# One layer of a graph network on one core: the filters' transforms cut into eight small products side by side, and the opening planned together with the odd products

## The chip, the cores and the metric

One core of a Trainium2 chip. The metric is device time in microseconds (us) of one execution; the time of a kernel is the median of several runs. The core has five engines with one instruction stream each: TensorE (PE in the profile; its weight loads are PEld), VectorE (DVE), ScalarE (ACT), GpSimd (POOL) and SyncE (SP). Each stream runs in the order in which it was written. Transfers are started by SP, ACT or POOL and run on 16 DMA engines.

## The reference

All data are float32. `x` is (64, 256, 256): 64 graphs of 256 nodes with 256 features. Cut to what matters:

```python
h = maximum(layernorm(x), 0)
# ref(h, adj, weights):
c = relu(bn1(conv1x1(h^T)))                    # 256x256
c = bn2(conv1d(c, conv2_w, padding=8))         # 17 taps, 256x256 channels, along the 256 nodes
x_conv = relu(c + h^T)^T
s = h @ w_se.T + b_se                          # 3 numbers a node
A = exp(-|s_i - s_j|^2) * adj
x_nmp = A @ relu(h @ w_msg.T + b_msg)
g = GRU cell (input [x_conv, x_nmp], state h)  # w_ih (768 x 512), w_hh (768 x 256)
out = x + g
```

## The kernel before

**The work.** Graphs are taken in 32 pairs, four pairs to a block, eight blocks. For a pair the kernel computes hT (the normalized features, channels on partitions), the message product, the affinity matrix, their product, and the gates of the cell. The convolution of 17 taps is done once per block for its eight graphs, in a transformed domain: the 256 nodes are 16 groups of 16, and the transform along a group has 16 complex bins (made by additions on DVE, `Fft.odd` for the upper half of the tree and `Fft.even` for the lower). In each bin the convolution is a 256 x 256 product of channels, done with three real products (kinds 0, 1, 2), 47 products in all (bin 15 has two). Bins 0 to 7 are the odd ones: `begin(0..3)` and `complete(0..3)` do their 24 kinds. Bins 8 to 15 follow in `begin(4..7)` and `complete(4..7)`.

**The filters.** For these products the 17 taps of each of 256 x 256 filters must be transformed into 47 numbers. That is done once, in the opening, on TensorE: `points` holds the transform's constants, `taps` the filters as they lie in memory, and `filters` (before: lines 854 to 864) multiplies them. Seven input channels (KG = 128 // 17) stand together on 119 partitions, and `points` is block-diagonal for them. The 16 bins are done in three passes of 6, 6 and 4 bins, so one step gives 126 or 77 rows of 512 numbers; 19 groups of channels (the last with two) times three passes are 57 steps. Each step is two matmuls (one for each half of the input channels), one ScalarE copy out of PSUM to a ring of eight tiles `fo`, and one transfer to a DRAM tensor `filt`, one for each pass. SP and POOL take turns in starting the transfers. The products read their weights back from `filt`: `load_kinds` starts one transfer of 256 KB for each kind into nine slots `wb`, on SP; each finished product frees a slot and starts the next.

**The opening** before the first product is: load x for pairs 0 to 3 and the taps; `norm`, `transpose_h`, `conv1`, `split` for each of the four pairs, with some filter steps after each; `forward(0)` and `forward(1)`, the additions of the transform for the first and second half of the block, odd then even for each; filter steps; `message(0)`, `embed(0)`, `affinity(0)` among the rest of the filter steps. Two names recur below: `embed` makes zT, the operand with 9 rows in each 32-row quadrant, and `affinity` multiplies zT with itself, a matmul of 9 rows for each of four row groups. At the very start TensorE runs 24 products of zeros (WARM).

**What sets the order.** All these calls are recorded by `Recorder`, line 371, and not issued at once: every engine instruction has line 371 in the profile, so it is found by the tiles it touches. `emit` plans what has been recorded: a list scheduler with a cost for each instruction (in `record`) and due times that come from TensorE's order in the program, and then issues it. What is recorded after an `emit` comes after all of what was before it, on each engine. Before, the first `emit` stands after the last filter step, ahead of the loop over blocks; the second ends the kernel. The tiles of the opening (`stage`: taps, fo, points) are freed after the first `emit`, and the tiles of the loop (`late`: Yv, w_x, xnm, gn, tr, back, hh, halves) take their place.

**In the first block** the loop then does `begin(0)`, `begin(1)`, `complete(0)`, `complete(1)`, `fft.branch_back`, `begin(2)`, ... , `fft.odd_back`, `aggregate(0)`; then loads w_hh and w_ih on POOL and combines them in `weight_sums` (12 additions and changes of sign on DVE). `q_back`, `p_back` and `join` on DVE end the transform. The first product of the gates that needs the convolution is in the trace "acc<-Yv,w_ih".

Of the kernel before, what the change touches and what calls it, by code (L numbers as in the profile page):

```python
# [249 lines left out]
class Recorder:  # L250
# [83 lines left out]
    def record(self, engine, op, args, kw):  # L334
# [3 lines left out]
        n = 1  # L338
# [13 lines left out]
        elif engine == "tensor":  # L352
            cost = n / 597 + 0.006
            if op == "transpose":
                cost = out.shape[-1] / 1170
            elif args[1].shape[0] < 32:
                cost = 0.23
        elif engine == "vector":
            cost = {"bn_stats": 0.33, "bn_aggr": 0.07}.get(op, n / 960 + 0.07)
            if op == "tensor_mul" and n == 256:  # L360
                cost = 0.5
        elif engine == "scalar":
            cost = n / 1400 + (0.2 if op == "activation" else 0.12)
            if out.dtype == U16:
                cost = n / 860
            elif len(out.shape) == 3 and op == "activation" and n == 256:
                cost = 0.49
        else:
            cost = 1.1 if self.planned == 0 else 7.0 if ALU.pow in args else 2.0
# [117 lines left out]
def kernel(  # L487
# [53 lines left out]
    def keep(name, *dims):  # L541
        return const.tile([P, *dims], FP, name=name)
# [24 lines left out]
    st, mv, rstd, shift = (Ring(keep(f"{name}{k}", *dims) for k in range(2)) for name, dims in (  # L567
        ("st", (G * MC, 6)), ("mv", (G * MC, 2)), ("rstd", (G * MC,)), ("shift", (G * MC,))))
    SLOTS = 9
    WARM = 24  # L570
    slots = [keep(f"wb{k}", DC, D) for k in range(SLOTS)]
    aux = Ring(psum.tile([P, W], FP, name=f"aux{k}") for k in range(4))
    acc = Ring(psum.tile([P, 2, W], FP, name=f"acc{k}") for k in range(2))
# [4 lines left out]
    adjh = keep("adjh", 2 * MC * W // 2).bitcast(U16).rearrange("p (k w) -> p k w", w=W)  # L578
    IN = ("h", "xc", "xn")

    U, V = (Slots(t, GB * DC, L // 2, NW) for t in (Ut, Vt))
    PT, Sv, T = (Slots(t, GB * DC, L // 4, NW) for t in (PTt, Svt, Tt))
    Yu = V
# [63 lines left out]

    KG = P // TAPS  # L650
    NG = -(-P // KG)
    FULL = NG - 1
    MAIN = KG * TAPS // 16 * 16
    PARTS = [(0, FULL // 6), (FULL // 6, FULL // 3), (FULL // 3, FULL)]


    PASSES = [range(0, 6), range(6, 12), range(12, 16)]
    taps = stage.tile([KG * TAPS, NG, DC, D], FP, name="taps")
    evicted = Ring(stage.tile([P, W], FP, name=f"fo{k}") for k in range(8))
    bank_points = [filter_points(p, TAPS) for p in PASSES]  # L660
    points = [stage.tile([P, KG * f.shape[1]], FP, name=f"points{n}") for n, f in enumerate(bank_points)]

    def load_taps(dc, a, b, eng):
        v = c2_wT[dc * P + a * KG:dc * P + b * KG].rearrange("(g k) t o -> (k t) g o", k=KG)
        eng.dma_start(out=taps[:MAIN, a:b, dc, :], in_=v[:MAIN])

    def load_last_taps(dc, eng):
        v = c2_wT[dc * P:dc * P + FULL * KG].rearrange("(g k) t o -> (k t) g o", k=KG)
        eng.dma_start(out=taps[MAIN:KG * TAPS, :FULL, dc, :], in_=v[MAIN:])

    def load_last_group(dc, eng):
        last = c2_wT[dc * P + FULL * KG:(dc + 1) * P]
        eng.dma_start(out=taps[:last.shape[0] * TAPS, FULL, dc, :], in_=last.rearrange("k t o -> (k t) o"))

    def load_points(n, eng):
        f = bank_points[n]
        m = np.zeros((P, KG, f.shape[1]), np.float32)
        for k in range(KG):
            m[k * TAPS:(k + 1) * TAPS, k] = f
        eng.dma_start(out=points[n], in_=tc.nc.inline_tensor(m.reshape(P, -1), name=f"points{n}").ap())  # L680


    ROWS = {}
# [13 lines left out]
    nc.scalar.dma_start(out=w_c1, in_=c1_wT.rearrange("(k p) o -> p k o", p=P))  # L697
    for j in range(PB):
        load_x(j)
    load_points(0, nc.scalar)  # L700
    for dc, eng in ((0, nc.sync), (1, nc.scalar)):
        load_taps(dc, *PARTS[0], eng)
        load_last_taps(dc, eng)
    for n in range(1, len(PASSES)):
        load_points(n, nc.scalar)
    for part in PARTS[1:]:
        load_taps(0, *part, nc.sync)
        load_taps(1, *part, nc.scalar)
    load_last_group(0, nc.sync)
    load_last_group(1, nc.scalar)  # L710
    nc.first = None
    nc.gpsimd.memset(Z, 0.0)
    nc.gpsimd.memset(Z[:, 0, :, 2 * SE:KD], 1.0)
# [135 lines left out]

    filt = [dram.tile([P, f.shape[1], DC, D], FP, name=f"filt{n}") for n, f in enumerate(bank_points)]

    def filters(p, m, g, eng):

        kinds = filt[m].shape[1]
        size = min(KG, P - g * KG)
        for dc in range(DC):
            mm(p[:size * kinds, dc * D:(dc + 1) * D], points[m][:size * TAPS, :size * kinds],
               taps[:size * TAPS, g, dc, :], start=dc == 0, stop=True, skip_group_check=True)  # L860
        t = evicted()
        nc.scalar.copy(t[:size * kinds], p[:size * kinds])
        eng.dma_start(
            out=filt[m][g * KG:g * KG + size].rearrange("k t c o -> (k t) (c o)"), in_=t[:size * kinds])


    free = deque(range(SLOTS))
# [8 lines left out]
    def load_kinds(count=SLOTS):  # L876
        for _ in range(count):
            if not (free and pending):
                return
            n, kind = pending.popleft()  # L880
            WB.append((free.popleft(), n, kind))
            m = n // len(PASSES[0])
            nc.sync.dma_start(out=slots[WB[-1][0]], in_=filt[m][:, 3 * (n - PASSES[m][0]) + kind])


    def operands(n):
# [314 lines left out]
            nc.gpsimd.dma_start(out=row_tile(y, g), in_=rows(x, G * i + g), accum_op=ALU.add)  # L1201
            nc.gpsimd.dma_start(out=rows(out, G * i + g), in_=row_tile(y, g))

    FIRST = PARTS[1][1]
    steps = deque((m, g) for g in range(FIRST) for m in range(len(PASSES)))
    steps.extend((m, g) for m in range(len(PASSES)) for g in range(FIRST, NG))
    banks = [0]

    def filter_steps(n):
        for _ in range(n):  # L1210
            banks[0] += 1
            p = acc()[:, 0] if banks[0] % 3 == 0 else aux()
            filters(p, *steps.popleft(), nc.gpsimd if len(steps) % 2 else nc.sync)

    norm(0)
    bn1 = columns("bn1")
# [14 lines left out]
    for t, v in ((b_msg[:, :D], msg_b), (b_msg[:, D:], se_b)):  # L1231
        nc.gpsimd.dma_start(out=t, in_=bass.AP(tensor=v.tensor, offset=v.offset, ap=[[0, P], [1, v.shape[0]]]))
    nc.sync.dma_start(out=w_msg[:, :, :D], in_=msg_wT.rearrange("(k p) o -> p k o", p=P))
    load_adj(0, nc.sync)
    load_x(PB)
    forward(0)
    forward(1)
    filter_steps(len(steps) - (NG - FIRST) - 4)
    pending.extend(TURNS)
    load_kinds()  # L1240
    message(0)
    filter_steps(8)
    embed(0)
    filter_steps(4)
    affinity(0)
    filter_steps(len(steps))
    nc.emit()
    stage_ctx.close()
    late = ctx.enter_context(tc.tile_pool(name="late", bufs=1, reuse_waits="tile"))
    Yvt = late.tile([P, SL], FP, name="Yv")  # L1250
    Yv = Slots(Yvt, GB * DC, L // 2, NW)
    w_x = late.tile([P, 3, len(IN), 3, P], FP, name="w_x")
    xnms = Ring(late.tile([P, DC, W], FP, name=f"xnm{k}") for k in range(2))
    gn_tile, tr_tile = (late.tile([P, DC, W], FP, name=n) for n in ("gn", "tr"))
    back = late.tile([P, DC * W], FP, name="back")
    hh, halves = (late.tile([P, 2 * MC, W], U16, name=n) for n in ("hh", "halves"))
    for b in range(NB):
        i = b * PB
        nxt = i + PB
# [18 lines left out]
            norm(nxt)  # L1278
        fft.branch_back(Yv, T, 2)
        fft.odd_back(Yv, T)  # L1280
        aggregate(i)
        begin(4)
        begin(5)
# [159 lines left out]
```

## Time and profile before

| | us |
|---|---|
| median of 3 runs | 1715.54 |
| lowest and highest of these | 1710.89, 1717.69 |
| profiled execution, its own time | 1717.68 |
| span of its profile (first to last instruction) | 1715.9 |
| PE busy in the span | 1670.4 (97%) |
| DVE busy | 1462.3 (85%) |
| ACT busy | 1040.0 (61%) |
| PE's share of the chain that ended last | 81% |
| DVE's share of it | 11% |
| mean granted TensorE clock | 0.991 |
| first product of the block (acc<-Sv,wb) starts | 97.47 |
| first product of the gates on the convolution (acc<-Yv,w_ih) starts | 166.16 |

A matmul of float32 stands as two records in the trace[...] and a record's end is modelled, so that records overlap. What a matmul takes is read from the distance between starts: two 256-column matmuls, four records, start 0.86 us before the next thing. Times below are us from the span's start.

### The profile page before, as it was taken

Reading aid. Unit: us, or ns where it says so; the run is one execution under the profiler, and the core shown is the slowest. Engines: PE = TensorE matmul, PEld = TensorE weight load, DVE = VectorE, ACT = ScalarE, POOL = GpSimd, SP = SyncE. Lnnn points to the kernel's source line nnn. Section 1 sums busy time; section 2 is a strip of 40 time slices with the busy share of each in tenths; the row PEclk is TensorE's granted clock in tenths of the full one; section 3 lists DMA queues with packets and bytes.
Section 4 is the critical chain, followed back from the end, with each engine's and each line's share of the span. In section 5 each row is a group of like instructions: output and inputs, shape, how many; then the busy total and the mean of one; then the engine's idle time right before and its main releaser. Section 6 shows DMA issues by size and latency. Waiting matters only on the chain.

```text
span 1715.9 us, 26176 instructions
## 1 busy us (share of the span) xinstructions
PE 1670.4 (97%) x8998; PEld 1418.1 (83%) x8998; DVE 1462.3 (85%) x3400; ACT 1040.0 (61%) x1949; POOL 229.8 (13%) x246
## 2 busy tenths in 40 slices
PE   8999999999999999999999999999999999999996
PEld 5788878988789788888888887897888988898885
DVE  7969989798897898898987988978988889879553
ACT  3545665576656756576655766567566665557543
POOL 3210021012110221102110031102211021100000
PEclk9999999999999999999999999999999999999998
DMA  9883665885568465784568645794758846374122
GB/s 217 263 267 121 124 129 117 279 157 127 111 167 254 103 142 99 231 207 97 120 115 271 153 98 119 157 272 99 139 106 218 225 91 135 62 251 113 24 51 50
DMA packets 326457, 260.90 MB, mean 152 GB/s; under 512 B 204808, under 2 KB 252196, under 8 KB 326323
## 3 DMA queue, kind: packets, MB, share of 16 engines
q1 hardware_dynamic: 293818, 213.72, 48.2%
q0 software_dynamic: 29568, 42.84, 13.5%
q10 hardware_dynamic: 2937, 2.66, 0.7%
q8 instruction: 71, 1.16, 0.3%
q14 instruction: 63, 0.52, 0.1%
HBM read 156.03 MB, written 43.78 MB: 116 GB/s over the span
## 4 chain that ended last, share of the span: by engine, by line
PE 81%; DVE 11%; DMA 4%; ACT 3%; issue 1%; POOL 0%; SPq 0%; ACTq 0%; DVEq 0%; POOLq 0%
PE acc L371 56%; PE aux L371 25%; DVE V L371 2%; DVE T L371 2%; DVE tr L371 1%; DVE U L371 1%; DMA wb<-filt 1%; DMA filt<-fo 1%; DMA hh<-halves 1%; ACT gn L371 1%; DVE acc L371 1%; ACT zT L371 1%; DVE e L371 1%; DVE Yv L371 1%; DVE gn L371 1%
## 5 line engine op out<-in xcount | busy, mean ns | idle before, releaser
L371 PE MATMUL acc<-wb,w_ih 128*128 128x256 f32 x768 | 192.4, 379 | 0.0
L371 PEld LDWEIGHTS acc<-wb,w_ih 128*128 128x128 f32 x768 | 145.9, 190 | 19.8
L371 POOL DMA_DIRECT2D back<-in_x_dram x62 | 61.8, 1154 | 717.1 <-ACT back L371 713.8
L371 PE MATMUL acc<-wb,w_x 128*128 128x256 f32 x576 | 137.5, 383 | 11.5 <-DVE acc L371 11.5
L371 PE MATMUL aux<-wb,w_x 128*128 128x256 f32 x576 | 141.9, 384 | 2.3 <-ACT e L371 2.3
L371 DVE SCALAR_TENSOR_TENSOR V<-T,V 128x128 f32<-128x128 f32 (+2 forms) x448 | 140.6, 375 | 0.0
L371 PEld LDWEIGHTS acc<-wb,w_x 128*128 128x128 f32 x576 | 107.3, 190 | 38.1 <-DVE acc L371 19.8
L371 POOL TENSOR_TENSOR rstd<-rstd,neg_half 128x4 f32<-128x4 f32 x32 | 76.9, 2404 | 442.7 <-DVE shift L371 251.3
L371 PEld LDWEIGHTS aux<-wb,w_x 128*128 128x128 f32 x576 | 107.8, 191 | 22.4 <-ACT e L371 4.3
L371 PE MATMUL aux<-w_msg,hT 128*128 128x259 f32 x512 | 121.1, 381 | 2.7 <-ACT fo L371 2.7
L371 PE MATMUL acc<-V,wb 128*128 128x128 f32 x1024 | 117.7, 275 | 0.9 <-DMA wb<-filt 0.9
L371 PEld LDWEIGHTS acc<-U,wb 128*128 128x128 f32 x1024 | 117.1, 192 | 0.9
L371 PE MATMUL acc<-U,wb 128*128 128x128 f32 x1024 | 117.2, 275 | 0.0
L371 PEld LDWEIGHTS acc<-V,wb 128*128 128x128 f32 x1024 | 116.0, 192 | 1.3 <-DMA wb<-filt 1.3
L371 ACT COPY back<-gn 128x1024 uint16<-128x1024 uint16 x62 | 81.0, 1348 | 54.1 <-DMA gn<-back 54.1
L371 PE MATMUL acc<-Yv,w_ih 128*128 128x256 f32 x384 | 110.1, 382 | 0.9 <-ACT Yv L371 0.8
L371 PEld LDWEIGHTS aux<-w_msg,hT 128*128 128x128 f32 x512 | 96.3, 189 | 17.5 <-ACT fo L371 3.1
L371 PE MATMUL acc<-wb,w_hh 128*128 128x256 f32 x384 | 109.9, 381 | 0.0
L371 PE MATMUL aux<-hT,w_c 128*128 128x512 f32 x224 | 105.4, 594 | 2.1 <-DVE msg L371 1.6
L371 PE MATMUL acc<-hT,w_hh 128*128 128x256 f32 x384 | 105.9, 383 | 0.7 <-ACT acc L371 0.7
L371 PE MATMUL aux<-e,msg 128*128 128x256 f32 x448 | 104.4, 379 | 0.0
L371 PE MATMUL acc<-xnm,w_ih 128*128 128x256 f32 x384 | 104.4, 380 | 0.0
(179 smaller groups left out, 3768.0 us busy)
## 6 DMA issues: line engine op xcount, KB each, us to landing
wb<-filt SPq DMA_DIRECT2D x376, 256.0 KB
back<-in_x_dram POOLq DMA_DIRECT2D x62, 256.0 KB, 7.8
out_dram<-back POOLq DMA_DIRECT2D x62, 256.0 KB, 4.8
x<-in_x_dram SPq DMA_DIRECT2D x58, 256.0 KB
halves_d<-halves SPq DMA_DIRECT2D x28, 512.0 KB
adjh<-halves_d SPq DMA_DIRECT2D x112, 128.0 KB
hh<-halves SPq DMA_DIRECT2D x108, 128.0 KB
filt<-fo SPq DMA_DIRECT2D x18, 252.0 KB
```

The source lines that it names most:

```text
L371: self.tasks.append(Task(engine, lambda: method(*args, **kw), cost, size, self.first))
```

## The change

- The filters' transforms. The taps now lie with their 17 taps on partitions, four times (RG = 4) at partitions 0, 32, 64 and 96; quarter r holds 16 input channels (PIECE) of channels 64r to 64r + 63. There are four pieces in a ring of two tiles. A step takes four channels of each quarter: eight matmuls with 17 rows, 64 output rows (47 used and one spare are kept, the rest are zeros) and 512 columns; each has its own quarter of rows and its own half of the output partitions. All 16 bins are done in one step, so 16 steps replace 57. The results go to one `acc` (two banks) and two `aux` banks.
- Ahead of the eight, each step has one full 128 x 128 product of 512 columns of w_c1 with itself. Its result is overwritten. It waits for all that the eight wait for.
- The copies out of PSUM: one of 1024 columns and two of 512 a step, in place of one of 512 for each old step. Four transfers of 192 KB a step, from 48 partitions each, two on SP and two on POOL, in place of one of up to 252 KB. The ring of eight tiles is made of `e_tile`, `adjh`, four quarters of Yv, and two tiles of its own.
- `filt` is one DRAM tensor, so a load of any kind depends on the last step's rows.
- The taps' loads: for each piece four transfers of 16 partitions x 16 KB on SP, and four of one partition x 16 KB on ACT or POOL, in place of transfers of 112 and of 7 partitions. Pieces 2 and 3 are loaded when a tile is free.
- The transforms of the data are recorded odd for both halves, then even for both; all filter steps that are left stand ahead of `message(0)`.
- `load_adj(0)` and `load_x(PB)` are planned after the loads of the first nine kinds. After `affinity(0)` six full products of w_c1 with itself follow.
- The first `emit` is moved into the loop's first pass, after `odd_back`: the odd products are planned with the opening. Yv becomes a tile of its own from the start.
- The plan's cost of a matmul of fewer than 32 rows becomes 0.13 where its output isn't 256 wide. WARM goes from 24 to 35.

```diff
-    KG = P // TAPS
...
+    RG = P // Q
+    HALF = P // 2
+    PIECE = 16
+    KINDS = 3 * BINS
+    taps = Ring(stage.tile([P, PIECE, D], FP, name=f"taps{k}") for k in range(2))
+    lent = [e_tile.rearrange("p g c n -> p (g c n)"), adjh.rearrange("p k w -> p (k w)").bitcast(FP)]
+    lent += [Yvt[:, k * 2 * W:(k + 1) * 2 * W] for k in range(4)]
...
+    def load_taps(eng=nc.gpsimd):
+        t, a = taps(), len(PIECES) * PIECE
+        for r in range(RG):
+            v = c2_wT[r * HALF + a:r * HALF + a + PIECE].rearrange("k t o -> t k o")
+            nc.sync.dma_start(out=t[r * Q:r * Q + L], in_=v[:L])
+            eng.dma_start(out=t[r * Q + L:r * Q + TAPS], in_=v[L:])
+        PIECES.append(t)
...
-    def filters(p, m, g, eng):
-
-        kinds = filt[m].shape[1]
-        size = min(KG, P - g * KG)
-        for dc in range(DC):
-            mm(p[:size * kinds, dc * D:(dc + 1) * D], points[m][:size * TAPS, :size * kinds],
-               taps[:size * TAPS, g, dc, :], start=dc == 0, stop=True, skip_group_check=True)
-        t = evicted()
-        nc.scalar.copy(t[:size * kinds], p[:size * kinds])
-        eng.dma_start(
-            out=filt[m][g * KG:g * KG + size].rearrange("k t c o -> (k t) (c o)"), in_=t[:size * kinds])
+    filt = dram.tile([P, KINDS, DC, D], FP, name="filt")
+
+    def filters(n):
+
+        k, first = n * 4, len(nc.tasks)
+        t, ps, fs = PIECES[k // PIECE], [], []
+        for h in range(2):
+            ps.append([aux(), aux()] if h else acc())
+            fs.append(evicted())
+        mm(ps[0][:, 0], w_c1[:, 0, :P], w_c1.rearrange("p k o -> p (k o)"), start=True, stop=True)
+        for h in range(2):
+            for c in range(DC):
+                rows_r = slice((2 * c + h) * Q, (2 * c + h) * Q + TAPS)
+                for q in range(2):
+                    mm((ps[h][c] if h else ps[h][:, c])[q * HALF:(q + 1) * HALF], points[rows_r],
+                       t[rows_r, k % PIECE + 2 * q:k % PIECE + 2 * q + 2].rearrange("t k o -> t (k o)"),
+                       start=True, stop=True, skip_group_check=True)
...
+        nc.scalar.copy(fs[0].rearrange("p k c o -> p c k o"), ps[0].rearrange("p c (k o) -> p c k o", k=2))
+        for c in range(DC):
+            nc.scalar.copy(fs[1][:, :, c], ps[1][c].rearrange("p (k o) -> p k o", k=2))
+        for h, f in enumerate(fs):
+            for q in range(2):
+                a = h * HALF + k + 2 * q
+                (nc.gpsimd if h else nc.sync).dma_start(
+                    out=filt[a:a + 2].rearrange("k s c o -> s k (c o)"),
+                    in_=f[q * HALF:q * HALF + KINDS].rearrange("p k c o -> p k (c o)"))
...
-    forward(0)
-    forward(1)
-    filter_steps(len(steps) - (NG - FIRST) - 4)
+    for kind in (0, 1):
+        for k in range(2):
+            forward(k, (kind,))
+    filter_steps(len(steps))
     pending.extend(TURNS)
     load_kinds()
+    nc.behind = nc.last["sync"]
+    load_adj(0, nc.sync)
+    load_x(PB)
+    nc.behind = None
     message(0)
-    filter_steps(8)
     embed(0)
-    filter_steps(4)
     affinity(0)
-    filter_steps(len(steps))
-    nc.emit()
...
+    p = aux()
+    for _ in range(6):
+        mm(p, w_c1[:, 0, :P], w_c1.rearrange("p k o -> p (k o)"), start=True, stop=True)
     for b in range(NB):
...
         fft.odd_back(Yv, T)
+        if b == 0:
+            nc.emit()
+            stage_ctx.close()
+            late = ctx.enter_context(tc.tile_pool(name="late", bufs=1, reuse_waits="tile"))
```

## Prediction

> **What bounds the kernel now.** I read the page's first part (PE 97%, DVE 85% of the span), then each engine's busy time by stretches of the opening, TensorE's timeline, the groups of instructions by form, and DVE's waits. Stretches first; columns are length, busy us of PE, PEld, DVE, ACT and POOL with counts, granted TensorE clock, busy share of the DMA engines, GB/s.
>
> ```profile
> 6.00:12.60 6.60, 3.98 (x35) 3.61 (x34) 3.19 (x13) 0.20 (x1) 4.38 (x9) 1.00 1.08 238
> 12.60:19.40 6.80, 6.23 (x13) 3.20 (x13) 5.80 (x27) 0.00 (x0) 3.52 (x6) 0.50 1.12 174
> ...
> 84.40:91.20 6.80, 6.59 (x28) 3.13 (x26) 6.48 (x24) 4.99 (x14) 1.57 (x3) 1.00 0.87 296
> 91.20:98.00 6.80, 6.80 (x21) 4.30 (x21) 4.44 (x17) 2.64 (x7) 1.80 (x3) 0.50 0.61 190
> 98.00:128.00 30.00, 30.00 (x235) 28.61 (x234) 18.34 (x35) 13.35 (x33) 3.11 (x4) 1.00 0.85 283
> 128.00:164.50 36.50, 36.15 (x255) 31.81 (x254) 36.22 (x76) 18.98 (x41) 1.30 (x2) 1.00 0.47 146
> 164.50:246.00 81.50, 80.12 (x363) 65.36 (x361) 78.61 (x185) 54.40 (x102) 13.43 (x12) 1.00 0.61 124
> ```
>
> Three things are to be seen. TensorE is nearly always busy, so work taken from it counts. It ran two stretches of 6.8 us at half clock, each with 3.4 us of work in it less than it could hold; before the second it was busy 6.59 of 6.80 us, but with products of 77 output rows. And from 128 to 246 DVE is as full as TensorE (36.2 of 36.5, 78.6 of 81.5): what TensorE gains in the opening is worth only what DVE can follow. DVE's busy time to 164.5 sums to 135.95 us, so it was idle 28.5 us. Its waits to 166, and TensorE's timeline:
>
> ```profile
> DVE msg L371 <- PE aux L371: 8.4, 3, 7.9
> DVE x L371 <- POOL rstd L371: 5.4, 1, 5.4
> DVE st L371 <- DMA x<-in_x_dram: 4.1, 2, 3.7
> DVE st L371 <- DMA T<-in_x_dram: 3.4, 2, 1.9
> DVE V L371 <- ACT h L371: 2.3, 1, 2.3
> ```
>
> ```profile
> 86.27 0.69 PE L371 MATMUL aux<-zT 9*128 9x256 f32 x2
> 86.89 1.09 PE L371 MATMUL acc<-taps,points 119*77 119x256 f32 x4
> ...
> 90.10 0.70 PE L371 MATMUL aux<-zT 9*128 9x256 f32 x4
> 90.73 0.66 PE L371 MATMUL acc<-taps,points 34*22 34x256 f32 x2
> ...
> 96.62 1.06 PE L371 MATMUL aux<-taps,points 119*77 119x256 f32 x2
> 97.47 2.20 PE L371 MATMUL acc<-Sv,wb 128*128 128x128 f32 x16
> ```
>
> The second list (start, length, records; two records a matmul) says that the first product follows the last filter matmul at once: weights were there, TensorE's own work was not done. It also prices small row groups: one zT matmul takes 0.62 us to the next start, two take 0.63.
>
> [...] at 352.32 us four zT matmuls take 0.65 us[...] One zT matmul alone takes 0.62 us where one of 256 columns in full rows takes 0.43 (0.86 for two). [...] the rate fell to 123 GB/s (8 to 10.4 us), against 282 in the 3 us before. [...]
>
> **The change, part by part.**
>
> *Filters on TensorE.* Removed: 57 steps x 2 matmuls x 0.43 us = 49.0 us. Added: 16 full products x 0.86 (twice 0.43) = 13.8 us, and the small ones. Eight at once would take two halves of 0.43 us (half of a full one's 0.86) and what the zT group pays over a full 256-column matmul, 0.65 - 0.43 = 0.2, or half of that for 64 weight columns in place of 128: 0.96 to 1.07; I take 1.0. If column halves do not overlap it is 2.0, if nothing does 6.9. But the built order shows early groups pulled apart: in nine steps, between conv1 and transposes, small ones stand in pairs or alone, about 19 groups; the last ten steps' worth stand as five pairs, about 10 groups. Each group pays 1.0 whatever it holds: 29 us. Six more full products after the affinity: 5.2 us. Sum 48.0, nearly what was removed. Both half-clock stretches gone would save 6.8 us; the longer warm-up (11 x 0.22 = 2.4 us) lies in the wait for x and closes most of the hole behind the first. A new stretch of small lone products can bring one back. So TensorE's own gain is 49.0 + 6.8 - 48.0 = 7.8 us; bounds: 3.4 us less for every new half-clock stretch.
>
> *When products can start.* conv1(0) ends at 20.7 before; now two small products stand ahead of it that need taps at about 16 us, with a faster clock after: 20.5. From there TensorE has conv1(1..3) 12 x 0.86 = 10.3, transposes 24 x 0.11 = 2.7, full 13.8, groups 29: 76.3. Waits for ScalarE's copies (per step about 0.92 + 2 x 0.49 = 1.9 us, just above TensorE's half of a pair) and for the third and fourth piece of taps: I add 4, so filters end at 80. Then, where messages and affinity formerly lay beside filters, they stand alone: message 3.5, DVE and ScalarE 1.7, z 0.4, zT's copies 2.6 (3.8 from z to zT before, shared with other copies), zT 0.6, six full products 5.2. Products start at 94, 3.5 us earlier. The six hide the write and reload of the last filters; without cover that would be 6.0 (landing of filt) + 3 = 9, to 89 + ScalarE 2 = 91.
>
> *DMA.* [...] By 85 us some 20 MB must have moved, 235 GB/s on average; before, 0 to 97.5 moved 239. So DMA is close to binding[...].
>
> *Odd products planned with the opening.* Before, 24 odd kinds took 97.5 to 128.7, because aggregate, message(1), transposes and zT stood between; now they are alone: 24 x 0.91 = 21.9 us (64 records in 7.3 us before, 8 kinds). Last Yv at 94 + 21.9 + 1.2 = 117. Then DVE: second branch 7.0, odd_back 7.7, and 27 to the scaling of the first xc, relu: 160 against 166.2 for the first gate product on the convolution. DVE alone: it needs 135.95 - 6.2 (nine operations, most of weight_sums, now stand behind that point in its order) = 129.7 of work, plus idle: 11 to the first conv1, 14 waiting for conv1(1..3), which TensorE now reaches some 17 us later because filter groups stand between, 1 for POOL's power: 156. So the products bind by a little, not DVE.
>
> *What is late next.* The 6.2 us of weight sums are then still to do and the gates need them; TensorE covers some with its first gate products (some 12 matmuls before w_x is needed in full); I charge 1 to 6, take 1.5. So 166.2 - 160 - 1.5 = 4.7, say 5 us. After 166 the same work is left and both engines are full, so nothing gives it back.
>
> POOL gets 32 filter writes in place of 28 and 8 taps loads (0.53 us each): hidden, POOL is 13% busy. SP's load_adj(0) and load_x(4) wait behind the loads of weights; the affinity's multiplication then stands ahead of nothing urgent. w_hh and w_ih are loaded some 5 us later on POOL, 15 us ahead of their use.
>
> **Sum.** Profiled execution: 1717.7 - 5 = 1712.7. The median stood 2.1 below it: 1710.5, rounded to 1710.
>
> **Rivals.** (1) *More is gained*: [...] conv1 comes as early as before, so DVE idles only 11 + 3 + 1 and TensorE's products start at 88. For it: TensorE's gain was computed with every lone product paying in full. [...] Gates at 150 to 153, 10 to 16 us earlier: 1702. (2) *DMA becomes the bound, slower*: [...] every product needs the last step's rows. It decides once the last write lands after 99 us (then products start after 101, the first gates after 167); at 109[...], the gates start near 175: 1723. For it: the drop to 123 GB/s. [...] (3) *Column halves do not run side by side*, or clocks halve twice more: 14 or 7 us on TensorE, products at 101 to 108: 1715 to 1724.
>
> **How the numbers follow.** Forecast 0.43 (1706 to 1714), rival 1 0.32, rival 2 0.14, rival 3 0.11. About 0.5% (8.6 us) is what a measurement of this kernel can tell from no change. Faster by more: most of rival 1 and the forecast's edge, 0.38. Slower by more: the far half of rivals 2 and 3, 0.17. Same: 0.45. Range 1697 to 1725: rival 1 to its end, rival 2 to its price, with one in ten left on each side.
>
> **What would show it.** Right: eight small records start within some 0.1 us where they stand together, 1.0 us a group; no half-clock stretch before 98; acc<-Sv,wb near 94, acc<-Yv,w_ih near 160 with DVE full between 85 and 160. Wrong: small groups at 2 us; filt landing after 99; conv1 of the fourth pair before 45 us (rival 1); DVE waiting for Yv by more than 8 us.

## The result, and the profile after

The kernel after takes 1764.6 us (median of 4 runs, 1760.74 to 1766.59) against 1715.1 before: a ratio of 1.0288, 95% interval [1.0261, 1.0316]. It is slower by 49 us, where 1710 had been forecast. Its profiled execution took 1760.74 us, with a span of 1759.0.

| us from the start | before | predicted | after |
|---|---|---|---|
| conv1 of the fourth pair ends | 39.7 | some 57 | 73.6 |
| last filter product starts | 97.0 | ends 80 | 109.2 |
| first product (acc<-Sv,wb) | 97.5 | 94 | 127.2 |
| last odd product ends | 128.2 | 116 | 156.5 |
| first gate product (acc<-Yv,w_ih) | 166.2 | 160 | 203.4 |
| end of the profiled execution | 1717.7 | 1712.7 | 1760.7 |

The loss is made in the opening: 29.8 us by the first product and 37.3 by the first gate product, of 43.1 between the two profiled executions. First the stretches of the kernel after, as in the prediction (length, then busy time of PE, PEld, DVE, ACT and POOL, the granted clock, DMA share, GB/s):

```profile
12.60:19.40 6.80, 4.82 (x20) 2.19 (x19) 6.43 (x26) 0.59 (x1) 3.33 (x7) 1.00 1.17 119
20.00:40.00 20.00, 20.00 (x58) 6.60 (x56) 9.90 (x22) 6.22 (x9) 3.13 (x6) 0.74 0.68 107
40.00:60.00 20.00, 20.00 (x56) 5.45 (x55) 7.74 (x12) 6.71 (x10) 2.83 (x6) 0.66 0.30 80
60.00:80.00 20.00, 20.00 (x93) 7.03 (x86) 12.45 (x37) 7.96 (x13) 4.97 (x9) 0.83 0.88 173
...
98.00:128.00 30.00, 25.87 (x111) 12.53 (x110) 20.48 (x69) 13.13 (x31) 6.61 (x12) 0.80 0.69 206
128.00:164.50 36.50, 31.63 (x254) 29.83 (x253) 20.63 (x45) 10.08 (x18) 3.84 (x5) 1.00 0.94 308
164.50:246.00 81.50, 81.22 (x431) 67.85 (x430) 77.39 (x162) 51.74 (x110) 9.60 (x8) 0.98 0.38 101
```

The early hole is shut: the clock is 1.00 from 12.6 to 19.4, where it was 0.50. But from 20 to 80 us TensorE is busy all the time at a clock of 0.66 to 0.83, and the others are largely idle. From 40 to 60 us it has 56 records, DVE is busy 7.7 of 20 us, and DMA's share is 0.30. Before, the same 20 us were:

```profile
40.00:60.00 20.00, 20.00 (x93) 16.24 (x91) 19.94 (x65) 13.41 (x23) 6.27 (x12) 1.00 0.75 206
```

TensorE is full and does little. What DVE waits for in the kernel after, up to 203 us, says the same (in total, times, longest):

```profile
DVE V L371 <- ACT h L371: 28.7, 3, 12.3
DVE T L371 <- ACT Yv L371: 10.3, 2, 9.3
DVE e L371 <- DMA adj<-in_adj_dram: 6.8, 2, 5.9
```

It waited 28.7 us for conv1 (h), 2.3 before. TensorE's timeline of the kernel after shows why (start, length, records; two records a matmul). The clock stood at half from 24.9 to 35.2 us and from 42.0 to 55.6:

```profile
23.35 1.07 PE L371 MATMUL aux<-taps,points 17*64 17x512 f32 x2
24.35 0.33 PE L371 MATMUL aux<-ident,T 128*128 128x128 f32 x1
...
27.29 1.97 PE L371 MATMUL aux<-taps,points 17*64 17x512 f32 x4
...
43.10 0.47 PE L371 MATMUL aux<-ident,Sv 128*128 128x128 f32 x1
43.50 1.96 PE L371 MATMUL aux<-taps,points 17*64 17x512 f32 x2
45.40 0.47 PE L371 MATMUL aux<-ident,Sv 128*128 128x128 f32 x1
45.80 1.96 PE L371 MATMUL aux<-taps,points 17*64 17x512 f32 x2
...
117.33 2.86 PE L371 MATMUL aux<-zT 9*128 9x256 f32 x8 [0.77 <-ACT zT L371]
120.12 7.28 PE L371 MATMUL aux<-w_c 128*128 128x512 f32 x12
127.23 1.95 PE L371 MATMUL acc<-Sv,wb 128*128 128x128 f32 x16
```

One small product alone between two transposes takes 1.9 us at half clock from its start to the next start; two together (27.29) take the same. At full clock one alone takes 1.0 us (23.35 to 24.35), and a whole group of eight no longer (0.86 us in e10 below). The last lines show the tail: the six full products stand right ahead of the first product, for 7.1 us.

The next table gives TensorE's time up to the first product, by kind, for the kernels before and after and three of the experiments below. Each record counts from its start to the next start, at most for its length; TensorE's first record starts at 1.8 us.

| us | before | after | e1: whole groups | e16: no full ones | e9: both |
|---|---|---|---|---|---|
| filter products | 53.1 | 41.3 | 23.1 | 43.9 | 32.7 |
| full products that serve nothing | 0 | 24.3 | 29.6 | 0 | 0 |
| conv1 | 16.4 | 21.5 | 16.1 | 21.3 | 17.2 |
| warm-up, transposes, message, zT | 20.1 | 26.0 | 23.1 | 25.3 | 24.7 |
| idle | 6.1 | 12.3 | 10.9 | 14.5 | 13.2 |
| first product starts | 97.5 | 127.2 | 104.6 | 106.8 | 89.6 |
| of the time up to it at half clock | 13 | 48 | 38 | 61 | 42 |

### The profile page after: what moved, and what is told of

It reads as the page before. It is cut to its first block, busy times and chain, and to the rows that moved or that the text cites. A ratio compares the mean times of both kernels' runs of the same rounds, so it can differ in the third digit from the quotient of the medians.

```text
span 1759.0 us, 26374 instructions
## 1 busy us (share of the span) xinstructions
PE 1699.1 (97%) x9092; PEld 1404.4 (80%) x9092; DVE 1462.9 (83%) x3400; ACT 1041.3 (59%) x1940; POOL 243.7 (14%) x258
## 4 chain that ended last, share of the span: by engine, by line
PE 72%; DVE 11%; DMA 5%; ACT 3%; issue 2%; SPq 1%; POOL 0%; ACTq 0%; DVEq 0%
PE acc L371 51%; PE aux L371 21%; DVE V L371 3%; DMA wb<-filt 2%; DVE T L371 2%; DMA hh<-halves 2%; DVE tr L371 1%; DVE U L371 1%; DVE e L371 1%; ACT zT L371 1%; ACT gn L371 1%; DVE acc L371 1%; SPq L371 1%; DVE Yv L371 1%; ACT hT L371 1%
## 5 line engine op out<-in xcount | busy, mean ns | idle before, releaser
L371 POOL TENSOR_TENSOR rstd<-rstd,neg_half 128x4 f32<-128x4 f32 x32 | 80.5, 2516 | 449.9 <-DVE shift L371 271.1
L371 PEld LDWEIGHTS aux<-w_msg,hT 128*128 128x128 f32 x512 | 96.0, 189 | 16.4 <-ACT Yv L371 1.0
L371 DVE TENSOR_TENSOR T<-Yv 128x512 f32<-128x512 f32 (+1 forms) x80 | 42.5, 581 | 75.4 <-ACT Yv L371 74.9
```

The costliest lines, as they stand in the source:

```text
L371: self.tasks.append(Task(engine, lambda: method(*args, **kw), cost, size, self.first))
```

## The experiments

The theory at the outset: the planner tears the groups apart, small products that stand alone take 1 us each and halve the clock, and so conv1 and with it DVE come late. Rivals: the taps' transfers bind (A), the serial tail from the last filter to the first product binds (B), the moved plan costs (C).

**e1, whole groups.** The planner gets the full product and its eight small ones as a chain that it issues without a break.

```diff
+            if k in self.glue:            # in commit
+                j = self.glue[k]
+                at = next(at for at, q in ready[e] if q == j)
+                commit(j, e, at, max(free[e], at))
...
             nc.tasks[first].preds.update(p for p in nc.tasks[j].preds if p < first)
+            nc.tasks[j].preds.add(j - 1)
+            nc.glue[j - 1] = j
```

> The kernel after, with one thing changed: the full product and its eight small ones are planned as one unit, so that nothing stands between them on TensorE. Theory (small products torn apart by the planner fill TensorE with 1 to 2 us records that use a corner of the array, the clock halves, and conv1 of the later pairs comes late): at most two half-clock stretches in the opening in place of six, conv1 of the fourth pair ends by 60 us (73 after), first product on Sv by 115 (127), time about 1748, between 1740 and 1754. Rival A (the taps' transfers at 110 GB/s bind): conv1 comes earlier but the filters still end near 109, time 1760 to 1767. Rival B (the serial tail from the last filter write to the first product binds): filters end by 98, products still 18 us later, near 115. Rival C (the moved plan boundary costs): within 4 us of 1765.

Measured: 1727.15 us, 1.0061 [1.0038, 1.0084] of before. Conv1 of the fourth pair starts its last matmul at 51.5 us and the first product comes at 104.6. With whole groups 37 of the 49 us come back, more than the theory had forecast. The last filter product starts at 86.4, 18 us ahead of the first product; that tail, rival B's, is as long as in the kernel after, and is not what came back. Yet the clock was not as expected: it stood at half from 59.9 to 90.6, in whole groups with a full product between. The timeline of e1:

```profile
59.67 1.92 PE L371 MATMUL acc<-w_c 128*128 128x512 f32 x2 [2.96 <-ACT fo L371]
...
63.69 2.08 PE L371 MATMUL acc<-w_c 128*128 128x512 f32 x2
65.69 1.13 PE L371 MATMUL acc<-taps,points 17*64 17x512 f32 x4
65.72 1.13 PE L371 MATMUL aux<-taps,points 17*64 17x512 f32 x4
66.60 1.08 PE L371 MATMUL acc<-taps,points 17*64 17x512 f32 x4
66.63 1.07 PE L371 MATMUL aux<-taps,points 17*64 17x512 f32 x4
67.63 2.08 PE L371 MATMUL acc<-w_c 128*128 128x512 f32 x2
```

A step (63.69 to 67.63) is 3.94 us with no gap in it, half of it the full product that should have kept the clock.

**e2, conv1 first.** The ten filter steps between the pairs' conv1 are moved behind the fourth.

```diff
-        filter_steps((1, 2, 3, 3)[j])
```

> The kernel after without the ten filter steps between the conv1 of the first four pairs: all sixteen stand behind conv1 of the fourth pair in the program's order. Theory: no small product stands before 30 us, conv1 of the fourth pair ends by 45 us as in the kernel before, VectorE has the odd transforms done by 75 (91 after); sixteen steps at 0.86 + 2 x 1.0 are 46 us, so the filters end near 92 to 100 and the first product starts near 112; time 1745 to 1755. Rival A: the first two pieces are there by 30 us in any case and the third and fourth now load during the filters, which end no earlier than 109; 1760 or more. Rival C: 1762 to 1768.

Measured: 1761.68 us, 1.027 [1.0239, 1.0301]. A miss: conv1 ended early as expected (last matmul at 32.8), but the filters then ran from 34.5 to 118.4 almost wholly at half clock (38.3 to 82.7, 86.1 to 123.7). Late conv1 is one way to lose; the filters' own length is another.

**e3 and e7, the taps over two queues.** In e3 quarters 0 and 1 go on one queue, 2 and 3 on the other, seventeen rows a transfer; in e7 each is still cut into sixteen rows and one.

```diff
-            nc.sync.dma_start(out=t[r * Q:r * Q + L], in_=v[:L])
-            eng.dma_start(out=t[r * Q + L:r * Q + TAPS], in_=v[L:])
+            q = (nc.sync, eng) if r < RG // 2 else (eng, nc.sync)     # e7
+            q[0].dma_start(out=t[r * Q:r * Q + L], in_=v[:L])
+            q[1].dma_start(out=t[r * Q + L:r * Q + TAPS], in_=v[L:])
```

> The kernel after with the taps' transfers dealt differently: the groups at partitions 0 and 32 on one queue, those at 64 and 96 on the other at the same time, each whole with its seventeen rows. [...] Rival A (these transfers bind): the rate between 12 and 25 us rises from 118 to over 200 GB/s, the filters end 8 to 15 us earlier, time 1748 to 1757. Theory (the clock, not the transfers): the rate rises but the torn groups stay, at least four half-clock stretches, time 1759 to 1767.

Measured: 1856.19 us, 1.0817 [1.0778, 1.0857]; it tells nothing of rival A. From 30 to 60 us, with transfers of seventeen rows on both queues, DMA's mean share was 0.07, about what one engine of sixteen makes, at 22 GB/s.

> The kernel after with the taps' transfers dealt over two queues at the same time, and each group's rows still in a transfer of sixteen and one of one (e3_taps_two_queues had seventeen rows in one[...] and measured that instead). Rival A (the taps' transfers bind): the rate between 12 and 25 us rises from 118 to over 200 GB/s, the filters end 8 to 15 us earlier, 1748 to 1757. Theory (the clock): the rate rises, the torn groups and at least four half-clock stretches stay, 1759 to 1767.

Measured: 1759.68 us, 1.0252 [1.023, 1.0274]. The time is the theory's. But its rate did not rise: 131 GB/s from 12.6 to 19.4 us, 119 in the kernel after. Nor did the two queues run side by side: from 13 to 15 us SP's moved 32 GB/s and ACT's 107, from 15 to 17 us 8 and 102, from 19 to 22 us 85 and 6. So this run did not take rival A's transfers away; e1 does more against A, with the same transfers and 37 us less.

**e4, the plan closed early** (the block with `nc.emit()` goes back ahead of the loop).

> The kernel after with the first plan closed before the first block, as in the kernel before, so that the odd products are planned with the later blocks again. Rival C (the moved plan boundary costs): the 7 us lost between the first product and the first gate product, and the 6 us lost over the later blocks, come back; 1750 to 1756. Theory: both are consequences of the late opening, except the last 6; 1758 to 1768.

Measured: 1761.67 us, 1.0272 [1.0238, 1.0305]: in the kernel after, rival C explains none of the 49 us that can be told.

**e5 and e6, the full product in front of each whole group:** none, and two.

```diff
-        mm(ps[0][:, 0], w_c1[:, 0, :P], w_c1.rearrange("p k o -> p (k o)"), start=True, stop=True)
```

> Whole groups as in e1_whole_groups, but without the full product in front of each of the sixteen steps (its result is used by nothing, so the output is computed in full). In e1_whole_groups the clock stood at half from 59.7 to 90.4 us while whole groups and full products alternated, a step taking 3.95 us. If the full product doesn't keep the clock, it only adds 1.9 us a step at half clock: the filters end 8 to 15 us earlier than 86.4 (or as early as transfers and ScalarE let them, some 2 us a step), time 1708 to 1722. If it keeps the clock for some of the time (the change's own reason), half clock begins before 45 us, conv1 of the third and fourth pair come late, time 1730 or more.

Measured: 1719.23 us, 1.0023 [1.0012, 1.0034], 8 us below e1. Half clock began at 37.7 us, in e1 at 59.9: one full product to a group seems to have held the clock for a while, and cost more than that was worth.

> Whole groups as in e1_whole_groups, with two full products in front of each step. If the clock follows the share of full products, two of them (1.7 us of a step of 2.7) hold it: no long half-clock stretch between 45 and 100 us, steps of 2.75 us in place of 3.95, time 1716 to 1724. [...] a step takes 2 x 2.7 = 5.5 us and the filters end some 12 us later than in e1_whole_groups: 1735 to 1745.

Measured: 1735.44 us, 1.0108 [1.0079, 1.0136]. The clock held from 20.5 to 81.9 us, as this stretch of e6 shows:

```profile
60.00:80.00 20.00, 17.45 (x117) 5.23 (x115) 18.23 (x59) 9.84 (x15) 9.27 (x15) 1.00 1.01 250
```

So its clock is the first forecast's (1.00 from 60 to 80 us), and its time is in the second's 1735 to 1745, 8 us above that with one. Two did keep the clock here; they cost more (38.9 us of full products up to the first product) than the clock is worth.

**e8, the longer warm-up alone** (the kernel before with WARM = 35).

> The kernel before with 35 in place of 24 warm-up products and nothing else of the change. The half-clock stretch from 12.65 to 19.4 us should go; conv1 of the first pair then ends near 18.5 to 20, and as VectorE waits for x at that time, 0 to 3 us come of it: 1711 to 1717, same as before within what can be told.

Measured: 1713.49 us, 0.9991 [0.9978, 1.0004]: no difference that can be told. In its profile the stretch of half clock at 12.65 is gone.

**e9, e16: no full products,** neither the sixteen nor the six, with whole groups (e9) and with groups that the planner may tear, as in the kernel after (e16).

> Whole groups, none of the sixteen full products between steps and none of the six behind the affinity. In e5_no_full_product the six ran at half clock from 86.2 to 94.6 us, 8.4 us on the way to the first product. If the last weights are there by then, the first product starts 5 to 8 us earlier, at 87 to 90, and the time falls by as much: 1711 to 1715. If the reload of the last filters (written by 74 to 80) or VectorE's odd transforms end last, nothing comes of it: 1717 to 1721.

Measured: 1720.12 us, 1.0031 [1.0016, 1.0045]. The first product came at 89.6, at the late end of the first forecast, and the median stayed where e5 was. TensorE waited 4.1 us there for the weights; in the kernel after, e1 and e5 it didn't wait for them. Once the full products are gone, the write and reload of the last filters end last.

> The kernel after without its 22 full products, groups torn by the planner as there. If the full products held some of the clock in the kernel after, it is slower than 1765; if they only cost, as in the whole groups (8 us there), it is faster: TensorE has 16 x 0.86 less at full and twice that at half clock, 1740 to 1757. Theory: faster, as lone products lose the clock with or without full ones elsewhere.

Measured: 1734.62 us, 1.0106 [1.0081, 1.013], faster than expected. The four kernels make a square:

| median, us | with 22 full products | without |
|---|---|---|
| groups torn | 1764.6 | 1734.6 |
| groups whole | 1727.2 | 1720.1 |

With torn groups taking the full products out saves 30 us, with whole groups 7. The square isn't quite clean: without the full products the planner made another order, with the small products in 13 unbroken stretches in place of 25 and 4 lone ones in place of 8, so part of the 30 us may be the order. The full products may have held some clock: up to the first product 48 us stood at half clock with them, 61 without, which is 6 us of work; their own length there was 24.3 us.

**e10 and e15, what loses the clock and what brings it back.** Both append strips of matmuls, with operands that are at hand, to the kernel before.

```diff
+    def group():
+        for t, r in ((big[:, 1], 0), (aux.tiles[0], 2), (aux.tiles[1], 1), (aux.tiles[2], 3)):
+            for q in range(2):
+                small(t, r, q)
```

> The kernel before, and behind its last output TensorE alone runs strips of matmuls, each strip behind 40 full products of 128 rows (its time is that much longer; the output is computed in full): 32 groups of eight small products on 17 rows; 20 times one full and a group; 16 times two full and a group; 24 lone small products; 20 times one full and one lone; 16 times two full and one lone. Theory: groups alone and lone products alone halve the clock some 10 us into their strip; one full to a group halves it too (as in e1_whole_groups), two hold it (as in e6_two_full_products); one full to one lone product, 0.86 us to 1.0, halves it as well. If it is gaps and waits between the products that halve the clock in the kernels, all strips stay at full clock, as nothing in them waits.

Each is one execution. The strips of e10, of which four of six are shown: groups alone; one full to a group; lone products, from when the clock fell; one full to a lone one:

```profile
1742.00:1769.50 27.50, 27.50 (x513) 11.31 (x512) 0.00 (x0) 0.00 (x0) 0.00 (x0) 1.00 0.01 2
1805.00:1846.00 41.00, 41.00 (x359) 10.32 (x358) 0.00 (x0) 0.00 (x0) 0.00 (x0) 1.00 0.00 1
...
1966.00:2000.00 34.00, 34.00 (x41) 8.81 (x39) 0.00 (x0) 0.00 (x0) 0.00 (x0) 0.50 0.00 0
2037.00:2077.00 40.00, 40.00 (x79) 9.37 (x78) 0.00 (x0) 0.00 (x0) 0.00 (x0) 1.00 0.00 0
```

Only lone products lost it (the mean from 1962.30 to 1966.00 us is 0.97, and from there on 0.50); the two strips with two full ones kept it too, at 1.00 for 46 and 45 us. Groups without a gap kept it, 0.86 us each, with nothing between them. So the theory's "small products halve the clock" was too simple, and e1's 30 us at half clock were still to be explained. e15 asks whether the clock remembers:

> The kernel before and, behind its last output, strips as in e10_clock_strip (the time is that much longer; the output is computed in full). Three strips start with the clock lost to ten lone small products: then 16 groups; 16 times one full and a group; 16 times two full and a group. Three start at full clock and are paced by ScalarE's copies of each group's results, as the filters are: 20 groups; 20 times one full and a group; 20 times two full and a group. Theory now: small groups keep a full clock where they are dense, but lose it where they wait for copies, and once it is lost neither groups nor one full to a group bring it back, two full do. So: the first two strips stay at half clock to their end (about 30 and 60 us), the third returns within some 7 us; of the paced ones the first halves, the second (gaps filled by the full product) holds. If the clock doesn't remember, the first two return to full clock within 7 us as well.

Its strips in order: groups alone after the clock was lost; one full to a group after it was lost; two full to a group, from 9.2 us after their start; groups paced by copies, from 4.8 us after their start; one full to a group, paced likewise:

```profile
1756.40:1785.50 29.10, 29.10 (x259) 12.99 (x257) 0.00 (x0) 0.00 (x0) 0.00 (x0) 0.50 0.00 1
...
1837.70:1901.90 64.20, 64.20 (x290) 13.82 (x290) 0.00 (x0) 0.00 (x0) 0.00 (x0) 0.50 0.00 1
...
1959.00:1999.00 40.00, 40.00 (x278) 12.36 (x278) 0.00 (x0) 0.00 (x0) 0.00 (x0) 1.00 0.00 1
...
2040.80:2100.00 59.20, 36.14 (x280) 6.03 (x280) 0.00 (x0) 20.04 (x35) 0.00 (x0) 0.50 0.00 1
2138.00:2186.00 48.00, 48.00 (x359) 13.71 (x358) 0.00 (x0) 22.24 (x38) 0.00 (x0) 1.00 0.00 1
```

The same mix, one full to a group, held a full clock for 48 us and never left half clock in 64 us: in these strips it depended on which it started from. Groups that waited for copies (TensorE busy 36.14 of 59.20 us) lost the clock, dense ones (27.50 of 27.50 us in e10) did not. e1 fits this: a wait of 2.96 us for a copy at 56.7 us, the clock at half from 59.9, and no way back before 90.6, some 3 us into the message's products in full rows.

**e11, e13, e17: what the moved plan is worth.** e11 is e9 with the plan closed early; e13 is the kernel before with the plan moved and WARM = 35; e17 is e11 with adj and x loaded ahead of the filters, as before.

> e9_no_fillers with the first plan closed ahead of the first block, as in the kernel before. Odd products planned with the opening are worth something if this is slower than e9_no_fillers; by the prediction's sum the odd products alone end some 8 us sooner, of which DVE's work lets 3 to 5 through: e9_no_fillers plus 3 to 5 us. If the moved boundary costs (rival C), it is 2 to 6 us faster than e9_no_fillers.

Measured: 1730.18 us, 1.0081 [1.0056, 1.0106], 10 us slower than e9. Its timeline shows TensorE waiting for the adjacency's transposes, whose load of adj stood on SP behind nine loads of weights, these behind the last filter's writes, and landed at 101.8:

```profile
102.43 1.41 PE L371 MATMUL aux<-ident,e 128*128 128x128 f32 x4 [14.78 <-DVE e L371]
```

> The kernel before, its filters as they were, with the two other parts of the change: the odd products planned with the opening, and 35 warm-up products. (To make room, the tiles that take the filters' copies are lent from Yv, which is kept from the start.) e11_no_fillers_early_plan lost 10 us against e9_no_fillers for want of the moved plan, and e8_warm35_alone gained 0 to 4. If the moved plan is worth as much beside the old filters, 1703 to 1709, faster than before; if the old filters already leave room for message, transposes and odd products together, as the prediction had it, 3 to 5 us: 1709 to 1713; if it is worth only what a late opening loses (rival C of another sign), 1714 to 1717.

Measured: 1723.67 us, 1.0043 [1.0025, 1.0061]: slower than before, against all three forecasts. DVE's wait for the odd products from 98 to 166 us, in e13 and then in the kernel before:

```profile
DVE T L371 <- ACT Yv L371: 15.4, 2, 9.6
...
DVE T L371 <- ACT Yv L371: 0.3, 1, 0.3
```

Before, DVE was busy 20.1 us from 100 to 130, 11.7 in e13: while the odd products ran, DVE added biases to messages, multiplied e by adj and did the weight sums. With the plan closed behind `odd_back`, all this stands behind `odd_back` in DVE's order.

> e11_no_fillers_early_plan (whole groups, no full products between, the first plan closed ahead of the first block) with adj and x loaded ahead of the filters' steps, as in the kernel before, in place of behind the loads of weights. In e11_no_fillers_early_plan TensorE stood idle 14.8 us for adj, which landed at 101.8, before the first product at 105.2; in e13_before_moved_plan VectorE stood idle 15.4 us for Yv, since the moved plan left it nothing else to do. If both readings are right, the first product starts near 90, VectorE works on message, adjacency and weight sums while the odd products wait for their loads, the first gate product starts near 158 to 162, and the time is 1705 to 1713, below both kernels or level with the kernel before. If the slow part is the filters' writes whatever the order, 1718 to 1724.

Measured: 1723.91 us, 1.0042 [1.0024, 1.006]. A miss: the first product came at 99.6, not near 90, and the time is that of the second forecast. It is 6 us better than e11, so adj's place was most of e11's loss; it isn't better than e9. Between e9 and e17, which differ in adj's place too, the plan's boundary makes no difference that can be told.

**e12, e14, other orders of e9:** all filter steps behind conv1 (e12), the last four beside the message and affinity (e14).

> e9_no_fillers with all sixteen filter steps behind conv1 of the fourth pair in the program's order. If VectorE's late start with the third and fourth pair (V from h at 38.0 and 50.9 us in e5_no_full_product, 35.8 and 42.0 before) sets the time, conv1 ends by 36 us, VectorE's odd transforms end 8 us sooner and 2 to 6 us are gained on e9_no_fillers. If ScalarE's copies and the filters' writes set it (they can start only at 36), the filters end at 75 to 85 and it is 0 to 10 us slower.

Measured: 1728.31 us, 1.0065 [1.004, 1.009], the second forecast. Conv1's last matmul started at 34.2 us, but the filters then ran to 86.6, from 40.3 on nearly all at half clock, and the first product came at 100.0.

> e9_no_fillers with the last four filter steps laid beside message, embedding and affinity as in the kernel before, adj and x loaded ahead of them, and the copies' ring without the tiles that the affinity writes (six in place of eight). Rival B (the serial tail of message and affinity between the last filter and the first product): the first product comes 5 to 10 us earlier than 89.6 if the loads of weights follow at once; else it stays, since these loads can start only behind the last step's writes, which now come later: 0 to 8 us slower. Theory: the second, 1720 to 1728.

Measured: 1727.74 us, 1.0076 [1.0046, 1.0105]; the first product came at 102.3, later than e9's 89.6, as the theory had it: the last filters landed at 94.2, and their reload took until 102.2. So this run moved rival B's tail and did not take it away. The tail's length is on record: from the last filter product to the first product 17.5 us after, 14 in the prediction, so that it explains some 4 of the 33 us by which the first product missed its forecast.

**e18, half of the odd kinds' weights.**

```diff
-            nc.sync.dma_start(out=slots[WB[-1][0]], in_=filt[:, 3 * n + kind])
...
+                nc.sync.dma_start(out=slots[WB[-1][0]][:, 0], in_=filt[:, 3 * n + kind, 0])     # the first 24
...
```

> e9_no_fillers with half of the weights of the first block's 24 odd kinds left out: each load brings the first 128 of 256 input channels (128 KB in place of 256), and each product uses these for both halves, with as many matmuls as before. The prediction counted the odd products at 24 x 0.91 = 21.9 us; in e9_no_fillers they take 30.3 us from the first to the first even product (89.6 to 119.9), and the chain there stands on loads of wb. If the loads bind, they now take 22 to 25 us, and the first gate product comes 4 to 8 us earlier than 161.9; time 1712 to 1717. If TensorE's own order or VectorE binds, they stay at 29 to 31 us and the time within 3 us of 1720.

Measured: 1719.18 us, 1.002 [1.0, 1.0039]. A miss, and the 30.3 us there was read too long: it holds 3.5 us of the aggregation. Without that the odd products take 26.8 us in e9 and 25.2 here, and the first gate product comes at 162.4, 161.9 in e9. So in these two profiles loads cost about 2 us, and the gates come no earlier for it.

## Why the prediction was wrong

**Filters on TensorE, the step that failed.** It said 48.0 us in all, at full clock; 65.6 were measured (41.3 small, 24.3 full). The price of a group was right at full clock (1.0 us for a lone product in the kernel after, 0.86 for eight in e10); there were 35 groups in place of 29. Count and price together make some 6 of the 17.6 us. The other 11.7 are the clock: 23.5 of the 65.6 us stood at half clock, where half of the time is lost. "Both half-clock stretches gone would save 6.8 us" stood in the sum, with "3.4 us less for every new half-clock stretch" only as a bound, which was left unused though the step itself named the lone products that would bring them. Up to the first product 48 us were at half clock, 13 before. TensorE was busy in 44 of the 48, so the clock alone is worth some 22 of the 33 us by which the first product was late; the prediction had put it at nothing.

At half clock a lone product cost 1.9 us (43.50 to 45.40 in the kernel after) and a full one 1.7 to 2.0 (2.0 in e1, 63.69 to 65.69), so the filler pays double just where it fails. The prediction priced the full products at 13.8 and 5.2 us and took what they were for, the clock, as had. Without them this kernel is 30 us faster.

The 22 us are worked out from the trace and not tested: no run held torn groups at full clock. And it is not by the clock that the experiments gave the time back: e9 still stood 42 us at half clock before its first product. They took work from TensorE: filters and full products take 32.7 us there, 65.6 after. Whether the planner would have kept the groups together with a higher price for a small product than 0.13 was not tried.

**When products can start.** Predicted 94, measured 127.2. Of the 33 us, 17.6 are the filters above; conv1, priced at full clock, took 7.7 more than its 13.8; the rest is idle time and the other kinds at half clock. "Conv1(1..3) some 17 us later" became 34 for the last, so DVE waited 28.7 us for it, not 14.

**The odd products alone, 21.9 us:** 29.3 from the first to the last, 4.7 of it in waits for weights and some 0.9 in transposes of e. That is 7.4 us more. **From the last Yv to the gates, 43:** 45.7. 33.2 + 7.4 + 2.7 is the 43 us by which the first gate product came later than forecast. The remaining 4.6 to the end of the profiled execution are within what executions of one kernel differ by.

**With the torn groups and the full products gone, the times come near those forecast, in part by luck.** e9's profile has the first product at 89.6, where the prediction had 91 without the six full products, the last Yv near 118 and the first gate at 161.9, where it had 117 and 160. But whole groups were cheaper than the prediction's torn ones, and the half clock took this back: 23.9 of the 32.7 us of filters. Even so its median is 5 us above that of before, not 5 below. The profiled execution of e9 took 1715.25 us, 2.4 less than that of before, and stands near the low end of e9's 22 runs (1714.04 to 1729.54). What the other runs pay is not in this profile and stays open.

**The moved plan** was credited with the odd products' earlier end and charged 1.5 us for the weight sums. In e13 the charge was some 9 us (1.0043 against e8's 0.9991). The waits above point to the reason: not only the weight sums but also message(1) and the adjacency had filled DVE's time.

**DMA.** How fast the taps would load was the author's estimate, and rival 2's 1723 rested on it. In the kernel after the rate was 119 GB/s from 12.6 to 19.4 us; what sets it isn't shown: in e7, which was to test it, the two queues took turns. "Decides once the last write lands after 99 us": it landed at 120, but behind the last filter product of 109, and TensorE went from the six full products to the first product without a gap. Up to there the transfers followed; they did not bind.

**The rivals.** Rival 3 had, as its second case, the right mechanism ("clocks halve twice more") at 7 us for two; there were five stretches between 20 and 125 us, of 7 to 14 us each. Its first case was wrong: column halves did run side by side (eight small products in 0.86 us in e10). Rival 1 was wrong for want of an early conv1, rival 2 for its cause.

## What to carry to other kernels

A group of small matmuls that run side by side has to be issued as one unit (here 1727.2 us whole, 1764.6 torn): the planner, which saw eight tasks, filled its gaps with them one by one, each at the whole group's price (1.0 us alone, 0.86 for eight). Price a filler that keeps the clock at half clock too, and against the work that it rescues; two in place of one did keep it here and were slower than none (1735.4 us against 1719.2). Before a plan's boundary is moved, list what each engine did in the wait that the move leaves empty: in e13 VectorE waited 15.4 us for Yv, 0.3 before.

## What the runs showed of the hardware

- In the strips of e10 and e15 the clock depended on its own past. Eight small products of 17 x 64 side by side, without gaps, held a full clock for 27 us (e10: 1.00) and did not lift a half one in 29 us (e15: 0.50); with one full product each, a full clock held for 48 us and a half one was not lifted in 64 us (e15). Two full products each lifted it in 9 us (e15: 0.50 from 1949.7 to 1959.0 us, then 1.00); forty full ones alone, between two strips of e10, lifted it within 37 us (0.50 up to 2000 us, 1.00 from 2037). In the strips that stayed at half TensorE was busy all the time (29.10 of 29.10 and 64.20 of 64.20 us), so the kind of work counted there. In the traces of the kernels before and after a half-clock stretch took 3.4, 6.8, 10.2 or 13.7 us, but for the last of each, which runs past the trace's end.
- In e10 a group of eight takes 0.86 us behind another group (27.50 us for 513 records, sixteen a group), and a full product with a group 2.06 (41.00 us for 359 records, eighteen a step). A full product with a lone small one takes 2.03 (40.00 us for 79 records, four a step), and a lone one behind another about 0.82 (3.70 us for nine records). All of this is at full clock, but for the last tenths of the 3.70 us. That eight took hardly longer with a full product than one did (2.06 and 2.03) shows that the column halves ran side by side.
- With taps' transfers of seventeen rows in e3 DMA's mean share was 0.07, at 22 GB/s (30 to 60 us); with sixteen rows and one the rate was 119 GB/s in the kernel after (12.6 to 19.4 us).
